# Values in tiles of 128 tokens, sent through DRAM, in the window attention of a four-layer image kernel

## The chip, the cores and the metric

The kernel runs on one core of one Trainium2 chip. The metric is the device time of one execution in microseconds (us), as a median over several runs. A core has several engines that run side by side and meet only at semaphores: TensorE (PE) for matmuls, VectorE (DVE), ScalarE (ACT), GpSimd (POOL), and SyncE (SP), whose queue here issues the transfers (DMA) between the memory of the chip (DRAM) and the core's own SBUF. Matmuls write to PSUM, which has eight banks. The profile shows PE's weight loads as a line of their own (PEld), and a float32 matmul as two records.

## The reference

Four images of 56 x 56 tokens with 256 channels go through four layers. Each adds to its input an attention-like function of the group-normalised input. Only layer 3 is touched by this change. It is an attention in windows of 7 x 7 tokens, on an image shifted by 3:

```python
xs = jnp.roll(x, (-3, -3), axis=(1, 2))
xw = (windows of 7 x 7).reshape(B * nW, 49, C)
qkv = xw @ qkv_weight.T + qkv_bias            # q, k, v: 8 heads of 32
attn = softmax(q * 32**-0.5 @ k.T + bias + mask)
out = (attn @ v) @ proj_weight.T + proj_bias
```

then windows and shift are undone and the result is added to `x`. Queries, keys and values of a token are a product of its 256 normalised channels with a 256 x 256 matrix each.

## The kernel before

The stream of activations lies in DRAM with channels first, and each layer reads it and writes the next. In layer 3 the unit of work is a row of eight windows: 8 x 49 = 392 tokens (`WC`), eight rows an image, 32 rows in all. All is float32, with the channels in two halves of 128 (`CC = 2`). What happens to a row `r`:

- `load` and `prepare(r)`: the row is loaded, and DVE normalises it (`normalise`, L940) into `xn`, permuted so that the tokens of a window are next to each other. Six small operations.
- `project_rows(r)`: keys and queries come from `project` (L946), with the weights held in PE and 392 tokens streamed past them; ACT empties their PSUM tiles (L1841, L1845). Values are made the other way round by `value_rows` (L963): 98 tokens, a pair of windows, are held as weights and the 256 columns of the value matrix are streamed, so that a pair's values have their tokens on partitions 0 to 97. Four such pieces a row, two to a PSUM tile; DVE adds the bias and writes them to `v` (L965).
- `quad(r, hq)`, two for a row, one for each four heads. In `attend_quads` a unit's `logits` (L998) go into PSUM; DVE adds the mask to one half of them (L1003), ACT takes exponentials (L1002, L1004), POOL multiplies the other half by its exponentiated mask (L1005). One unit later `products` (L1013) multiply by `v` and by ones. After that `done` divides: a reciprocal (L1864) and a scaling (L1866) on DVE.
- `project_out(r)`, two rows later: `project` with `w_p`, ACT adds the bias into `pr` (L1886), POOL adds it to the old `x` in `xr` (L1888), and the row is stored (`transfer`, L1801).

The order is written out by hand: layer 3 runs under a manual schedule in which PE, DVE, ACT and POOL take their instructions in the order of the program. Only SP's queue is ordered by the scheduler. The loop over units is

```python
for w in units:
    logits(w)
    done()
    w["fill"]()
    if held:
        products(held)
        done = held["done"]
    held = w
```

so that between the logits of a unit and the products of the one before, PE is given the filling work of `stream()`: for each half `hq` of row `r` one step of the output projection of row `r - 2`, then three of the six steps of `project_rows(r + 1)` (keys, queries, values, in this order), and in the second half `prepare(r + 2)`.

PSUM is full: logits take two tiles of two banks, products one of two banks, and all that goes through `ps_m` (projections, values, statistics) shares two tiles of one bank, which are given out in turn.

Of the kernel before, what the change touches and what calls it, by code (L numbers as in the profile page):

```python
# [24 lines left out]
FP = mybir.dt.float32  # L25
I32 = mybir.dt.int32
AF = mybir.ActivationFunctionType
ALU = mybir.AluOpType
# [3 lines left out]
NIMG = 4  # L32
S = 56
T = S * S
C = 256
P = 128
CC = C // P
HD = 32
# [10 lines left out]
WC = 8 * WN  # L49
# [782 lines left out]
def direct_blocks(ctx: ExitStack, tc: tile.TileContext, d: dict, watch):  # L832
# [3 lines left out]
    nc = tc.nc  # L836
    const = ctx.enter_context(tc.tile_pool(name="dconst", bufs=1))
    dram = ctx.enter_context(tc.tile_pool(name="ddram", bufs=1, space=bass.MemoryType.DRAM))
# [8 lines left out]
    def tokens_of(l, b, t0, n):  # L847
        return stream_of[l][b].rearrange("(h p) t -> p h t", p=P)[:, :, t0:t0 + n]
# [7 lines left out]
    bv0, bv2, bv3, baff, gamma, beta = (bc[:, i, :] for i in range(6))  # L856
# [14 lines left out]
    def psum_tile(tag, bufs, banks=1):  # L871
        shape = [P, 512] if banks == 1 else [P, banks, 512]
        return ps.tile(shape, FP, tag=tag, name="ps_" + tag, bufs=bufs)
# [3 lines left out]
    def ps_m():  # L877
        return psum_tile("m", m_bufs)
# [55 lines left out]
    def known(l, b):  # L934
        while (l, b) not in stats:
            pending.pop(0)()
        return stats[l, b]

    def normalise(dst, src, gst, h):
        nc.vector.tensor_scalar(dst, src, gst[:, h, 0:1], gst[:, h, 1:2], ALU.subtract, ALU.mult)  # L940
# [16 lines left out]
    def value_rows(v, a, n, xn, w, bias):  # L957

        pm = ps_m()
        for j in range(2):  # L960
            k = 2 * a + j
            for h in range(CC):
                nc.tensor.matmul(pm[:n, j * C:(j + 1) * C], lhsT=xn[:, h, k * n:(k + 1) * n],  # L963
                                 rhs=w[:, h, :], start=(h == 0), stop=(h == CC - 1))
        nc.vector.tensor_tensor(v[:, 2 * a:2 * a + 2, :], pm[:n, :].rearrange("p (j c) -> p j c", c=C),  # L965
                                bias[:n].rearrange("p (o c) -> p o c", o=1).to_broadcast([n, 2, C]), ALU.add)

    def seen(rs):

        w = watch[0][:, :rs.shape[1]]  # L970
        nc.gpsimd.tensor_tensor(w, w, rs, ALU.add)
# [129 lines left out]
    def lazily(make, i, n):  # L1101

        made = []
        return [lambda k=k: (made or made.extend(make(i)), made[k]()) for k in range(n)]
# [687 lines left out]
    def layer3(early, big, pool, brief):  # L1792
        def image_rows(wr):

            return [(0, 7, 7 * wr + 3)] if wr < 7 else [(0, 4, S - 4), (4, 3, 0)]

        def transfer(l, r, x, out):
            b, wr = divmod(r, 8)
            for i0, n, r0 in image_rows(wr):
                ends = x[:, :, i0 * S:(i0 + n) * S], tokens_of(l, b, r0 * S, n * S)  # L1800
                nc.sync.dma_start(out=ends[out], in_=ends[1 - out])  # L1801

        xs, xns, qkv, attns = {}, {}, {}, {}

        def load(r):
            xs[r] = early.tile([P, CC, WC], FP, tag="x", name="x3")
            transfer(3, r, xs[r], 0)

        load(0)
        w_qkv = weight(early, "wqkv3", 3 * C)  # L1810
        m3 = big.tile([98, 2, NH, 4 * 98], FP, name="m3l")
        nc.sync.dma_start(out=m3, in_=m3d.rearrange("p a h w k -> p a h (w k)"))
        w_p = weight(pool, "wp3", C)

        def parts(win, x):

            win = win.rearrange("p (w i j) -> p w i j", i=7, j=7)
            img = x.rearrange("p (r c) -> p r c", c=S)
            yield (win[:, 0:7].rearrange("p w i j -> p i w j"), img[:, :, 3:52].rearrange("p r (w j) -> p r w j", j=7))
            yield win[:, 7, :, 0:4], img[:, :, 52:56]  # L1820
            yield win[:, 7, :, 4:7], img[:, :, 0:3]

        def prepare(r):
            x = xs.pop(r)
            if r + 1 < NIMG * 8:
                load(r + 1)
            xn = xns[r] = early.tile([P, CC, WC], FP, tag="xn", name="xn3")
            for h in range(CC):
                for w, xv in parts(xn[:, h, :], x[:, h, :]):
                    normalise(w, xv, known(3, r // 8), h)  # L1830

        def project_rows(r):
            xn = xns.pop(r)
            qT = pool.tile([P, CC, WC], FP, tag="q", name="q3")
            kT = pool.tile([P, CC, WC], FP, tag="k", name="k3")
            v = pool.tile([98, 4, C], FP, tag="v", name="v3")
            qkv[r] = qT, kT, v

            def keys(m):
                pm = project(w_qkv, C + m * P, lambda h: xn[:, h, :], WC)  # L1840
                nc.scalar.activation(kT[:, m, :], pm, AF.Identity, bias=bk3[:, m:m + 1])  # L1841

            def queries(m):
                pm = project(w_qkv, m * P, lambda h: xn[:, h, :], WC)
                nc.scalar.activation(qT[:, m, :], pm, AF.Identity, bias=qbias[:, 2, m:m + 1], scale=SCALE)  # L1845

            def values(a):
                value_rows(v, a, 98, xn, w_qkv[:, :, 2 * C:], bv3)

            return [lambda f=f, m=m: f(m) for m in range(2) for f in (keys, queries, values)]  # L1850

        def quad(r, hq):
            b, wr = divmod(r, 8)
            qT, kT, v = qkv[r]
            box = {}

            def output(k, u):
                if k + u == 0:
                    box["o"] = psum_tile("o", 1, 2)
                return box["o"][:, k, u * 98:(u + 1) * 98]  # L1860

            def finish():
                rs = pool.tile([P, WC], FP, tag="rs", name="rs3")
                nc.vector.reciprocal(rs, box["o"][:, 1, :WC])  # L1864
                seen(rs)
                nc.vector.scalar_tensor_tensor(attns[r][:, hq, :], box["o"][:, 0, :WC], 1.0, rs, ALU.mult, ALU.mult,  # L1866
                                               accum_out=watch[2][:, 2 * r + hq:2 * r + hq + 1])

            def piece(u):
                sl = slice(u * 98, (u + 1) * 98)  # L1870
                return (lambda j: kT[hr(j), hq, sl], lambda j: qT[hr(j), hq, sl],
                        lambda j: v[:, u, (4 * hq + j) * HD:(4 * hq + j + 1) * HD], True, True)

            mk = m3[:, wr // 7, 4 * hq:4 * hq + 4, :]
            i = 2 * (NIMG * 8 + r) + hq
            return dict(pieces=[piece(u) for u in range(4)], nk=98, nq=98, width=WC, mask=mk[:, 0:2, :],
                        emask=mk[:, 2:4, :], sum=watch[2][:98, i:i + 1], o=output, first=no_step, done=finish)

        def project_out(r):
            x = pool.tile([P, CC, WC], FP, tag="xr", name="xr3")  # L1880
            transfer(3, r, x, 0)

            def step(m):
                pm = project(w_p, m * P, lambda h: attns[r][:, h, :], WC)
                pr = pool.tile([P, WC], FP, tag="pr", name="pr3")
                nc.scalar.activation(pr, pm, AF.Identity, bias=bp3[:, m:m + 1])  # L1886
                for w, xv in parts(pr, x[:, m, :]):
                    nc.gpsimd.tensor_tensor(xv, xv, w, ALU.add)  # L1888
                if m:
                    transfer(4, r, x, 1)  # L1890
            return [lambda m=m: step(m) for m in range(CC)]

        def stream():
            n = NIMG * 8
            for r in range(n):
                attns[r] = pool.tile([P, CC, WC], FP, tag="attn", name="attn3", bufs=3)
                rows = lazily(project_rows, r + 1, 6) if r + 1 < n else []
                out = project_out(r - 2) if r > 1 else []
                for hq in range(CC):
                    steps = out[hq:hq + 1] + rows[3 * hq:3 * hq + 3]  # L1900
                    if hq and r + 2 < n:
                        steps.append(lambda r=r: prepare(r + 2))
                    steps.append(step_stats)
                    w = quad(r, hq)
                    w["fill"] = lambda steps=steps: [f() for f in steps]
                    yield w

        prepare(0)
        prepare(1)
        for step in project_rows(0):  # L1910
            step()
        attend_quads(pool, stream())
        for r in range(NIMG * 8 - 2, NIMG * 8):
            for step in project_out(r):
                step()
# [114 lines left out]
```

## Time and profile before

| | |
|---|---|
| time, median of 3 runs | 4114.57 us (4113.07 to 4121.27) |
| span of the profiled execution | 4109.9 us |
| PE, DVE, ACT, POOL busy | 95%, 58%, 33%, 42% of the span |
| first logits of layer 3 | at 3567.07 us |
| one half of a row in layer 3's steady part | 8.25 us |
| value matmuls (L963), layers 2 and 3 | 1024 records, 250.0 us busy |

Layer 3 takes about the last 540 us. A line of a group or of the timeline names the line in the kernel, the engine, the operation, what is written and read with shapes, and then how long and how often. In square brackets, or after a second bar, stands how long the engine stood idle just before and whose end released it. The time on PE of a group in the timeline includes the tail of its last matmul, so distances between starts say more than the lengths.

### The profile page before, as it was taken

The numbers are of one execution on the slowest core, as the hardware profiler recorded it, in microseconds if no ns is written. First come the engines' busy times: TensorE is split into PE (matmuls) and PEld (weight loads), VectorE is DVE, ScalarE is ACT, GpSimd is POOL, SyncE is SP. The second block draws the span as 40 slices with busy tenths as digits, with TensorE's granted clock in tenths as the row PEclk, the third lists the DMA queues.
The fourth block names the chain that finished last, engine by engine and source line by source line (L and its number), as shares of the span: only waits on it lengthen the run. The fifth ranks groups of instructions, "written<-read, shape, count | busy, mean of one in ns | idle before, by whom it ended". The sixth has DMA issues, their size and how long they took to land. (4 is left out here: it accounts for less than half of the span.)

```text
span 4109.9 us, 92570 instructions
## 1 busy us (share of the span) xinstructions
PE 3910.4 (95%) x39191; PEld 2788.9 (68%) x39191; DVE 2381.8 (58%) x4437; ACT 1373.1 (33%) x2850; POOL 1741.2 (42%) x1883
## 2 busy tenths in 40 slices
PE   6899999899999999999999999997999999899998
PEld 4566666577777677776777677775666666666665
DVE  6777777734345434454344533444688887666665
ACT  2444545422222122221222212222554555444443
POOL 2566667621123211242112411123676777554544
PEclk9999999999999999999999999998999999999999
DMA  7344333210000100000000000003344443322221
GB/s 261 101 133 122 113 112 101 89 41 10 15 15 24 34 9 15 15 29 29 10 15 15 28 17 10 10 19 117 109 127 121 123 122 112 104 76 73 72 76 61
DMA packets 239794, 275.89 MB, mean 67 GB/s; under 512 B 22150, under 2 KB 231720, under 8 KB 238888
## 3 DMA queue, kind: packets, MB, share of 16 engines
q1 hardware_dynamic: 239082, 269.80, 21.1%
q8 instruction: 310, 5.08, 0.5%
q14 instruction: 114, 0.93, 0.1%
q10 hardware_dynamic: 288, 0.08, 0.0%
HBM read 190.29 MB, written 79.53 MB: 66 GB/s over the span
## 5 line engine op out<-in xcount | busy, mean ns | idle before, releaser
L1414 DVE TENSOR_TENSOR acc<-acc,ps_v 128x257 f32<-128x257 f32 x1104 | 457.2, 421 | 679.5 <-PE ps_v L1410 676.6
L1410 PE MATMUL ps_v<-xw,e 128*128 128x257 f32 x2400 | 666.4, 382 | 27.4 <-DVE acc L1414 17.2
L1405 PE MATMUL ps_o<-xw,at 128*128 128x257 f32 x2400 | 662.5, 380 | 0.0
L1377 PE MATMUL ps_s<-xnT,xd 128*128 128x512 f32 (+3 forms) x1456 | 622.0, 550 | 5.1 <-DVE xnT L1359 5.1
L1410 PEld LDWEIGHTS ps_v<-xw,e 128*128 128x128 f32 x2400 | 445.1, 189 | 193.2 <-issue 91.8
L1394 ACT COPY at<-ps_t 128x512 f32<-128x512 f32 (+3 forms) x360 | 184.8, 513 | 1054.4 <-PE ps_t L1391 1054.4
L1064 POOL TENSOR_TENSOR b<-e 126x336 f32<-126x336 f32 (+5 forms) x512 | 499.7, 997 | 12.1 <-ACT e L1052 4.1
L1405 PEld LDWEIGHTS ps_o<-xw,at 128*128 128x128 f32 x2400 | 455.5, 190 | 65.3
L1370 POOL TENSOR_SCALAR xd<-xnT,vec 128x128 f32<-128x128 f32 x200 | 122.2, 622 | 707.4 <-PE ps_s L1377 705.6
L946 PE MATMUL ps_m<-xn,w_wqkv 128*128 128x392 f32 x1024 | 375.5, 500 | 3.3 <-DVE xr L1693 2.5
L1055 POOL TENSOR_TENSOR e<-e,m0t 126x672 f32<-126x672 f32 (+3 forms) x128 | 238.7, 1865 | 280.7 <-ACT e L1054 267.9
L1377 PEld LDWEIGHTS ps_s<-xnT,xd 128*128 128x128 f32 x1456 | 245.1, 191 | 155.6 <-issue 138.8
L1055 POOL TENSOR_TENSOR e<-e,bias 119x784 f32<-119x784 f32 (+5 forms) x128 | 244.5, 1911 | 215.7 <-ACT e L1054 214.8
L1380 ACT ACTIVATE e<-ps_s 128x512 f32<-128x512 f32 (+3 forms) x364 | 200.8, 552 | 375.2 <-PE ps_s L1377 373.3
L976 ACT ACTIVATE no<-rs 128x168 f32<-128x168 f32 (+2 forms) x256 | 93.8, 367 | 624.7 <-DVE rs L1658 283.1
L1073 PEld LDWEIGHTS ps_o<-e,vp 124*32 124x32 f32 (+3 forms) x8192 | 177.1, 111 | 142.9 <-issue 93.5
L946 PEld LDWEIGHTS ps_m<-xn,w_wqkv 128*128 128x128 f32 x1024 | 188.2, 190 | 124.8 <-ACT pr L1886 17.3
L963 PE MATMUL ps_m<-w_wqkv,xn 128*98 128x256 f32 x1024 | 250.0, 388 | 8.2 <-DMA w_wqkv<-in_wqkv 7.0
L1073 PE MATMUL ps_o<-e,vp 124*32 124x112 f32 (+3 forms) x8192 | 240.2, 254 | 6.2 <-POOL e L1055 4.7
L940 DVE TENSOR_SCALAR xn<-x,gst 128x28 f32<-128x28 f32 (+5 forms) x368 | 204.8, 611 | 50.7 <-PE ps_m L946 26.9
L1052 ACT ACTIVATE e<-e 126x672 f32<-126x672 f32 (+5 forms) x256 | 219.4, 857 | 24.0 <-DVE e L1051 10.7
L965 DVE TENSOR_TENSOR v<-ps_m,bc 98x512 f32<-98x512 f32 (+1 forms) x184 | 126.2, 686 | 174.3 <-PE ps_m L963 98.3
(164 smaller groups left out, 6136.4 us busy)
## 6 DMA issues: line engine op xcount, KB each, us to landing
x<-xr SPq DMA_DIRECT2D x64, 392.0 KB
x<-in_x SPq DMA_DIRECT2D x53, 448.0 KB
xr<-x SPq DMA_DIRECT2D x60, 392.0 KB
x<-x SPq DMA_DIRECT2D x60, 392.0 KB
vd<-v SPq DMA_DIRECT2D x28, 448.0 KB
xr<-in_x SPq DMA_DIRECT2D x32, 392.0 KB
xr<-x SPq DMA_DIRECT2D x28, 448.0 KB
x<-xr SPq DMA_DIRECT2D x28, 448.0 KB
```

The source lines that it names most:

```text
L940: nc.vector.tensor_scalar(dst, src, gst[:, h, 0:1], gst[:, h, 1:2], ALU.subtract, ALU.mult)
L946: nc.tensor.matmul(pm[:, :n], lhsT=w[:, h, col:col + P], rhs=rhs(h), start=(h == 0), stop=(h == CC - 1))
L963: nc.tensor.matmul(pm[:n, j * C:(j + 1) * C], lhsT=xn[:, h, k * n:(k + 1) * n], rhs=w[:, h, :], start=(h == 0), stop=(h == CC - 1))
L1052: nc.scalar.activation(ev, ev, AF.Exp)
L1055: nc.gpsimd.tensor_tensor(parts(ev), parts(ev), w["emask"], ALU.mult)
L1064: nc.gpsimd.tensor_tensor(w["b"][a][:nk, :, :2 * nq].rearrange("p h (i c) -> p h i c", i=2), ev[:, :, :, 0, :], ev[:, :, :, 1, :], ALU.add)
L1073: nc.tensor.matmul(w["o"](k, i)[j * HD:(j + 1) * HD], lhsT=ones[:nk, :HD] if k else v(j, u), rhs=w["b"][j // 2][:nk, j % 2, i * nq:(i + 1) ...
L1377: nc.tensor.matmul(s[:, :n], lhsT=xd[j][:, h, :], rhs=xnT[:, h, first * P:last * P], start=(h == 0), stop=(h == CC - 1))
L1380: nc.scalar.activation(e[:, :n], s[:, :n], AF.Exp, scale=5.0)
L1405: nc.tensor.matmul(out[j][:, :C + 1], lhsT=e[:, col(i)] if i == j else at[:, col(i)], rhs=xw[:, i, :], start=(i == j), stop=(i == NB - 1))
L1410: nc.tensor.matmul(pv[:, :C + 1], lhsT=e[:, col(i)], rhs=xw[:, j, :], start=True, stop=True)
L1414: nc.vector.tensor_tensor(acc[:, i, :], acc[:, i, :], pv[:, :C + 1], ALU.add)
```

## The change

Values are no longer made for each pair of windows but for tiles of 128 tokens, which fill the 128 columns of PE's weights. Since a row has 392 tokens, which isn't a multiple of 128, the tiles run on over the rows of an image: 25 for 3136 tokens, the last of 64. What a row leaves over (`left`: up to 120 tokens) is copied by ACT to the front of the next row's `xn`, which grows to 448 tokens and to three buffers. A tile of values has other tokens on its partitions than a pair of windows needs, so it is stored to a DRAM buffer `vd3` by token, and `gather` loads a row back as four pairs of 98 tokens into `v`. To leave time for this, values are made two rows ahead in place of one, and rows are prepared three ahead.

The filling work of a half changes in order as well: one step of the output projection, then one step of values (for row `r + 2`), then keys and queries (for row `r + 1`). The tile of values, `vt`, has one buffer. The core of the diff:

```diff
+    def value_tiles(v, a, c, n, xn, w, bias, dst):
+        t0, t1 = c * n // P, (c + 1) * n // P if (c + 1) * n < T else -(-T // P)
+        pm = ps_m()
+        sizes = [min(P, T - t * P) for t in range(t0, t1)]
+        mine = sizes[2 * a:2 * a + 2]
+        for j, k in enumerate(mine):
+            first = (2 * a + j) * P
+            for h in range(CC):
+                nc.tensor.matmul(pm[:k, j * C:(j + 1) * C], lhsT=xn[:, h, first:first + k], rhs=w[:, h, :],
+                                 start=(h == 0), stop=(h == CC - 1))
+        for k in sorted(set(mine)):
...
+            nc.vector.tensor_tensor(
...
+            nc.sync.dma_start(out=dst[t * P:min((t + len(js)) * P, T), :].rearrange("(k p) c -> p k c", p=k),
...
-            xn = xns[r] = early.tile([P, CC, WC], FP, tag="xn", name="xn3")
+            xn = xns[r] = early.tile([P, CC, 448], FP, tag="xn", name="xn3", bufs=3)
...
+            if at:
+                end = left(c - 1, WC) + WC
+                nc.scalar.copy(xn[:, :, :at], ahead[0][:, :, end - at:end])
...
-            return [lambda f=f, m=m: f(m) for m in range(2) for f in (keys, queries, values)]
+            return [lambda f=f, m=m: f(m) for m in range(2) for f in (keys, queries)]
+
+        def gather(r):
+            b, c = divmod(r, 8)
+            vs[r] = pool.tile([98, 4, C], FP, tag="v", name="v3")
+            nc.sync.dma_start(out=vs[r], in_=vd[b][c * WC:(c + 1) * WC, :].rearrange("(k p) c -> p k c", p=98))
+
+        def values(r):
...
+            v = pool.tile([P, 4, C], FP, tag="vt", name="vt3", bufs=1)
+            def step(a):
+                value_tiles(v, a, c, WC, xn, w_qkv[:, :, 2 * C:], bv3, vd[b])
+                if a == 0 and r:
+                    gather(r - 1)
...
-                    steps = out[hq:hq + 1] + rows[3 * hq:3 * hq + 3]
-                    if hq and r + 2 < n:
-                        steps.append(lambda r=r: prepare(r + 2))
+                    steps = out[hq:hq + 1] + ahead_values[hq:hq + 1] + rows[2 * hq:2 * hq + 2]
+                    if hq and r + 3 < n:
+                        steps.append(lambda r=r: prepare(r + 3))
...
         prepare(0)
         prepare(1)
+        for r in range(2):
+            for step in values(r):
+                step()
         for step in project_rows(0):
             step()
+        prepare(2)
         attend_quads(pool, stream())
```

More of the change, by code (lines that the diff above doesn't have):

```diff
@@ L966, in value_rows, with left @@
                                 bias[:n].rearrange("p (o c) -> p o c", o=1).to_broadcast([n, 2, C]), ALU.add)
+    def left(c, n):
+        return c * n % P
+    def value_tiles(v, a, c, n, xn, w, bias, dst):
[9 more added lines that the diff above has]
+        for k in sorted(set(mine)):
+            js = [j for j, kj in enumerate(mine) if kj == k]
+            nc.vector.tensor_tensor(
+                v[:k, 2 * a + js[0]:2 * a + js[-1] + 1, :], pm[:k, js[0] * C:(js[-1] + 1) * C].rearrange("p (j c) -> p j c", c=C),
+                bias[:k].rearrange("p (o c) -> p o c", o=1).to_broadcast([k, len(js), C]), ALU.add)
+            t = t0 + 2 * a + js[0]
+            nc.sync.dma_start(out=dst[t * P:min((t + len(js)) * P, T), :].rearrange("(k p) c -> p k c", p=k),
+                              in_=v[:k, 2 * a + js[0]:2 * a + js[-1] + 1, :])
     def seen(rs):
@@ L1801, in transfer @@
                 nc.sync.dma_start(out=ends[out], in_=ends[1 - out])
-        xs, xns, qkv, attns = {}, {}, {}, {}
+        xs, xns, vs, qk, attns, ahead = {}, {}, {}, {}, {}, []
+        vd = [dram.tile([T, C], FP, name=f"vd3_{b}") for b in range(NIMG)]
         def load(r):
@@ L1826, in prepare @@
                 load(r + 1)
-            xn = xns[r] = early.tile([P, CC, WC], FP, tag="xn", name="xn3")
+            c = r % 8
+            xn = xns[r] = early.tile([P, CC, 448], FP, tag="xn", name="xn3", bufs=3)
+            at = left(c, WC)
             for h in range(CC):
-                for w, xv in parts(xn[:, h, :], x[:, h, :]):
+                for w, xv in parts(xn[:, h, at:at + WC], x[:, h, :]):
                     normalise(w, xv, known(3, r // 8), h)
+            if at:
+                end = left(c - 1, WC) + WC
+                nc.scalar.copy(xn[:, :, :at], ahead[0][:, :, end - at:end])
+            ahead[:] = [xn]
         def project_rows(r):
-            xn = xns.pop(r)
+            at = left(r % 8, WC)
+            xn = xns.pop(r)[:, :, at:at + WC]
             qT = pool.tile([P, CC, WC], FP, tag="q", name="q3")
             kT = pool.tile([P, CC, WC], FP, tag="k", name="k3")
-            v = pool.tile([98, 4, C], FP, tag="v", name="v3")
-            qkv[r] = qT, kT, v
+            qk[r] = qT, kT
             def keys(m):
@@ L1845, in queries @@
                 nc.scalar.activation(qT[:, m, :], pm, AF.Identity, bias=qbias[:, 2, m:m + 1], scale=SCALE)
-            def values(a):
-                value_rows(v, a, 98, xn, w_qkv[:, :, 2 * C:], bv3)
-            return [lambda f=f, m=m: f(m) for m in range(2) for f in (keys, queries, values)]
+            return [lambda f=f, m=m: f(m) for m in range(2) for f in (keys, queries)]
[4 more added lines that the diff above has]
+        def values(r):
+            b, c = divmod(r, 8)
+            xn = xns[r]
+            v = pool.tile([P, 4, C], FP, tag="vt", name="vt3", bufs=1)
[3 more added lines that the diff above has]
+                    gather(r - 1)
+                if a and r == NIMG * 8 - 1:
+                    gather(r)
+            return [lambda a=a: step(a) for a in range(2)]
         def quad(r, hq):
             b, wr = divmod(r, 8)
-            qT, kT, v = qkv[r]
+            qT, kT = qk[r]
             box = {}
@@ L1871, in piece @@
                 return (lambda j: kT[hr(j), hq, sl], lambda j: qT[hr(j), hq, sl],
-                        lambda j: v[:, u, (4 * hq + j) * HD:(4 * hq + j + 1) * HD], True, True)
+                        lambda j: vs[r][:, u, (4 * hq + j) * HD:(4 * hq + j + 1) * HD], True, True)
             mk = m3[:, wr // 7, 4 * hq:4 * hq + 4, :]
@@ L1896, in stream @@
                 attns[r] = pool.tile([P, CC, WC], FP, tag="attn", name="attn3", bufs=3)
-                rows = lazily(project_rows, r + 1, 6) if r + 1 < n else []
+                rows = lazily(project_rows, r + 1, 4) if r + 1 < n else []
+                ahead_values = lazily(values, r + 2, 2) if r + 2 < n else []
                 out = project_out(r - 2) if r > 1 else []
                 for hq in range(CC):
-                    steps = out[hq:hq + 1] + rows[3 * hq:3 * hq + 3]
-                    if hq and r + 2 < n:
-                        steps.append(lambda r=r: prepare(r + 2))
+                    steps = out[hq:hq + 1] + ahead_values[hq:hq + 1] + rows[2 * hq:2 * hq + 2]
+                    if hq and r + 3 < n:
+                        steps.append(lambda r=r: prepare(r + 3))
                     steps.append(step_stats)
```

## The prediction

> **What bounds the kernel now.** I went from the whole to the one stage that the change touches. The page says that TensorE (PE) is busy 95% of the span. Busy time alone says little for a pipelined engine, so I cut out layer 3, which begins at about 3567 us, with the view by windows, once in its steady part and once at its end.
>
> ```profile
> PE 3910.4 (95%) x39191; PEld 2788.9 (68%) x39191; DVE 2381.8 (58%) x4437; ACT 1373.1 (33%) x2850; POOL 1741.2 (42%) x1883
> ```
> ```profile
> 3603.11:4072.00 468.89, 468.89 (x6576) 319.71 (x6576) 315.15 (x453) 195.20 (x342) 233.72 (x285) 1.00 0.22 72
> 4072.00:4110.00 38.00, 17.39 (x302) 11.73 (x290) 15.96 (x20) 6.84 (x12) 15.18 (x24) 0.83 0.21 66
> ```
>
> For 469 us PE has no idle time at all, at full clock (1.00), while VectorE (DVE) has 315 us of work and the DMA engines are 22% busy. So layer 3 is bound by the number and length of its matmuls. One half of a row (one step of the stream, one `hq`) in the timeline of PE, then the same stretch on DVE; columns are start, length, engine, line, operation, count, and the idle time before with what ended it:
>
> ```profile
> 3602.24 0.95 PE L998 MATMUL ps_s<-q,k 32*98 32x98 f32 x32
> 3603.11 1.58 PE L946 MATMUL ps_m<-attn,w_wp 128*128 128x392 f32 x4
> 3604.53 2.80 PE L946 MATMUL ps_m<-xn,w_wqkv 128*128 128x392 f32 x8
> 3607.17 1.89 PE L963 MATMUL ps_m<-w_wqkv,xn 128*98 128x256 f32 x8
> 3608.99 0.89 PE L1013 MATMUL ps_o<-e,v 98*32 98x98 f32 x32
> ```
> ```profile
> 3603.29 0.97 DVE L1003 TENSOR_TENSOR e<-ps_s,m3l 98x784 f32<-98x784 f32 x1 [0.90 <-PE ps_s L998]
> 3604.18 2.60 DVE L1864 RECIPROCAL rs<-ps_o 128x392 f32<-128x392 f32 x1
> 3606.81 0.56 DVE L1866 SCALAR_TENSOR_TENSOR attn<-ps_o,rs 128x392 f32<-128x392 f32 x1
> 3607.30 0.08 DVE L1866 DVE_READ_ACCUMULATOR attn<-ps_o,rs 128x1 f32 x1
> 3609.09 0.69 DVE L965 TENSOR_TENSOR v<-ps_m,bc 98x512 f32<-98x512 f32 x1 [1.71 <-PE ps_m L963]
> ```
>
> Call L the moment when the filling work begins on PE (3603.11 here). PE does output projection (L to L+1.42), keys and queries (to L+4.06), values (to L+5.88); then products and the next logits take 2.37, and the half is 8.25 us long. DVE, in the order written, does the mask, the reciprocal, the scaling of the previous unit (through at L+4.27), and only then the bias-add that empties the values' PSUM tile. Today the values come last on PE, at L+5.88, so DVE is long free: it waits 1.71 us for PE, not PE for it.
>
> Two more views. The waits, in the same stretch:
>
> ```profile
> PEld ps_m L946 <- ACT pr L1886: 17.0, 57, 0.3
> ```
>
> That is the queries' first weight load waiting until the output projection's tile, two back in `ps_m`, is emptied: the two buffers go round in turn, and the third project of a half waits for the first. And the last row, which has no filling work but the output projection:
>
> ```profile
> 4073.17 1.58 PE L946 MATMUL ps_m<-attn,w_wp 128*128 128x392 f32 x4
> 4077.59 0.89 PE L1013 MATMUL ps_o<-e,v 98*32 98x98 f32 x32 [2.83 <-DVE attn L1866]
> ```
>
> There L is 4073.17, and PE stands still until L+4.42 for the very DVE chain above. So this chain is only some 1.5 us away from being the bound.
>
> **What the Trainium skill says.** "Perfetto Trace Analysis", Sequencer Loop: an instruction of an engine goes into that engine's queue and there waits for its semaphore. In this trace what stands behind it in program order waits too (the 2.83 us above). The same page, Identifying Performance Opportunities, says that a gap repeating on the engine that should be saturated can mean that SBUF or PSUM had no room for the next tile. The trace of before shows the seed of it, the 0.3 us on `ps_m`. "TensorE: Matmul & The Clock Gate", LDWEIGHTS: a weight load's time goes with its columns. The trace agrees: 165 ns for 98 columns, 190 for 128. Both are below the 216 ns of a 256-wide matmul record with 128-column weights (L1349 in layer 1: 8 in 1.73 us), so wider tiles cost PE nothing each.
>
> **The change, part by part.**
>
> 1. Fewer value matmuls. An image has 32 pieces of 98 tokens now and 25 tiles of 128 afterwards, with two matmuls (two records each) per piece. That removes 14 matmuls an image, 56 in all. One is 2 x 213 ns (8 records in 1.71 us), so PE has 56 x 0.427 = 24 us less to do. By row: 3 tiles in place of 4, two in the first half and one in the second; each eighth row keeps 4.
>
> 2. The order in the filling. Values now stand second, right behind the output projection, and keys and queries follow. With two `ps_m` buffers, keys take over the output's tile and queries that of the values. So queries wait for DVE's bias-add, which DVE, in order, can't start before L+4.27. Behind that wait on PE stand queries, then products, then the next logits, hence the next mask and reciprocal: the loop closes, and the wait comes in every half.
>  - First half: values matmuls end at about L+3.1, keys at L+4.45. Bias-add L+4.26 to L+4.95 (98x512 took 0.69). A released weight load starts 0.06 later (layer 2's releases by DVE show that). Queries after a stop take 1.42, as the output projection does after logits, to L+6.43; with the 0.11 that PE now loses going into the products, the filling ends at L+6.54 instead of L+5.88: +0.66 us.
>  - Second half: one tile of 256, whose add I take from layer 1's 128x257 at 421 ns. 4.26 + 0.42 + 0.06 + 1.42 + 0.11 = L+6.27: +0.39 us.
>  - A row: +1.05 us, with the saved matmuls already inside, since the wait swallows them. Rows 2 to 29 do this: 28 x 1.05 = 29.4. In four rows the second half makes two tiles, of 128 and 64 tokens, with two adds of about 0.4: 4 x 0.34 = 1.4.
>
> 3. The ends. Row 0 has no previous unit in its halves at first, so no reciprocal ahead of the add, and gains its second half's tile: -0.9. Row 1 has no output projection yet, so its filling is 4.86 us now (half 7.23) and 6.54 and 6.27 afterwards: +3.1. Row 30 makes no values any more and becomes like the last row, L+4.42 instead of 5.88, twice: -2.9. Before the stream, two rows of values are made instead of one. The second row's tile has one buffer (`bufs=1`), so its first add waits until the first row's store has landed; I take 3.7 us for that, as an `xr` load of layer 2 near its end does. The first logits then start at about 3571.3 instead of 3567.07: +4.2.
>
> 4. DMA. Each row stores up to 512 KB and loads 392 KB back. Stores in layer 3 take 2.6 to 4.2 us to land (the queue's waits for `out_x`). A store goes out at L+5, the next row's add into the same buffer is due one half (9 us) later or more. The load is issued more than a half before its first use. Traffic doubles from 22% busy. So I cost it at nothing: attention's matmuls of the next halves hide it. The queue itself waits in order, and a store may stand behind the output's, which waits for GpSimd; that goes into the range.
>
> 5. The copy of left-over tokens: 28 copies on ScalarE of at most 128x240; a 128x512 copy there took 513 ns (L1394), so under 0.5 us each. ScalarE is busy 195 of 469 us and does it after the queries' eviction: nothing. The third `xn` buffer and normalising one row earlier move work without adding any. DVE's old wait for products before it may overwrite `v` (2.56 us in every other half) goes, but it held up no one on PE.
>
> Sum: 29.4 + 1.4 - 0.9 + 3.1 - 2.9 + 4.2 = +34 us. 4114.6 + 34 = 4149 us.
>
> **The rivals.**
>
> A. PE's count alone decides (the order does no harm, the DMA is hidden). That needs queries free by L+4.45. For it: 469 us without idle. Against it: the DVE chain shown by the last row, and only two `ps_m` buffers. Time: 4114.6 - 24 + 4 (start) = 4095. Chance 0.09.
>
> B. As forecast, and the one-buffer value tile bites as well: the store is stuck behind the output's store in the DMA queue, and each row's first add waits about 1 us more. For it: the queue waits 345 us for GpSimd's `xr` in layer 3. Against it: a full half of slack. 30 rows x 1 us more: 4179. Chance 0.12.
>
> C. The stall is smaller than worked out, with PE making up part of it, and the two cancel: within 8 us of before, at 4115. It would need the add to start 0.7 us sooner in both halves. Chance 0.05.
>
> **How the numbers follow.** My forecast has 0.74. Its own spread is that of the half (0.2 us each way, 60 halves: 12 us) and of the start (2 us less if the store lands at once). The range 4118 to 4172 takes that and the near side of B, and leaves out A, C and the far side of B. Faster 0.09, same 0.05, slower the rest, 0.86.
>
> **What would show it.** Right: in the steady part of layer 3 a half is 8.9 and 8.7 us by turns, PE idles 0.4 to 0.9 us in each, ended mostly by the values' bias-add on DVE ahead of an L946 matmul; value records in layer 3 fall from 512 to 400. Step 4 right: no DVE wait on a DMA of `vd`. Wrong: halves of 8.25 and 7.4 us (A), DVE's bias-add waiting for the store (B), or a long wait ahead of the first products for `v3`.

## The result: slower by 0.75%

| | before | after |
|---|---|---|
| median of 6 runs | 4113.82 us (4104.31 to 4121.27) | 4144.27 us (4137.72 to 4150.95) |
| ratio, 95% interval | | 1.0075 (1.0059 to 1.009) |
| first logits of layer 3, in the profile | 3567.07 | 3573.68 |
| from these to the last logits | 512.0 | 538.8 |
| from the last logits to the end | 30.8 | 29.3 |

The profile after, in the same two views as before. First a window of the steady part of layer 3, in the kernel before and then after (stretch, its length, then busy time and count for PE, PEld, DVE, ACT and POOL, then granted clock, DMA share and GB/s):

```profile
3620.00:4050.00 430.00, 430.00 (x6037) 293.20 (x6036) 289.40 (x418) 179.22 (x315) 213.57 (x261) 1.00 0.23 74
```
```profile
3620.00:4050.00 430.00, 405.28 (x5600) 263.38 (x5600) 274.65 (x392) 170.15 (x314) 202.62 (x245) 1.00 0.38 116
```

PE now idles for 24.7 of 430 us at full clock, in a stretch in which it never stood still before. In this window it had 6037 matmul records done before and has 5600 now; the value records that are saved explain only a part of that. Second, a row on PE. The first six lines are a second half (L is 3697.94), the next five the first half of the row after it (L is 3706.66); L983 is the line of the value matmuls now:

```profile
3697.94 1.58 PE L946 MATMUL ps_m<-attn,w_wp 128*128 128x392 f32 x4
3699.36 1.03 PE L983 MATMUL ps_m<-w_wqkv,xn 128*128 128x256 f32 x4
3700.51 1.58 PE L946 MATMUL ps_m<-xn,w_wqkv 128*128 128x392 f32 x4
3702.77 1.58 PE L946 MATMUL ps_m<-xn,w_wqkv 128*128 128x392 f32 x4 [0.68 <-ACT k L1874]
3704.29 0.89 PE L1039 MATMUL ps_o<-e,v 98*32 98x98 f32 x32
...
3705.78 0.95 PE L1024 MATMUL ps_s<-q,k 32*98 32x98 f32 x32
3706.66 1.58 PE L946 MATMUL ps_m<-attn,w_wp 128*128 128x392 f32 x4
3708.08 1.89 PE L983 MATMUL ps_m<-w_wqkv,xn 128*128 128x256 f32 x8
3709.81 1.48 PE L946 MATMUL ps_m<-xn,w_wqkv 128*128 128x392 f32 x4
3711.59 1.58 PE L946 MATMUL ps_m<-xn,w_wqkv 128*128 128x392 f32 x4 [0.30 <-DVE vt L987]
3713.10 0.89 PE L1039 MATMUL ps_o<-e,v 98*32 98x98 f32 x32
```

Queries, the fourth group of each half, wait. In the first half DVE's bias-add releases them at L+4.93, in the second ACT's eviction of the keys, at L+4.83. The DVE queue in the first half shows why the add comes so late:

```profile
3706.83 0.97 DVE L1029 TENSOR_TENSOR e<-ps_s,m3l 98x784 f32<-98x784 f32 x1 [2.13 <-PE ps_s L1024]
3707.72 2.60 DVE L1914 RECIPROCAL rs<-ps_o 128x392 f32<-128x392 f32 x1
3710.36 0.57 DVE L1916 SCALAR_TENSOR_TENSOR attn<-ps_o,rs 128x392 f32<-128x392 f32 x1
3710.85 0.08 DVE L1916 DVE_READ_ACCUMULATOR attn<-ps_o,rs 128x1 f32 x1
3710.85 0.69 DVE L987 TENSOR_TENSOR vt<-ps_m,bc 128x512 f32<-128x512 f32 x1
```

The values' matmuls are through at L+3.2, but the add stands fifth in its queue, behind a reciprocal of 2.60 us, without a gap between them. The halves are 8.82 and 8.72 us by turns, 17.54 us for a row that took 16.49. In every eighth row the second half makes two tiles and takes 8.94. What PE's weight loads (PEld) and its matmuls (PE) waited for in the window, in total, times and the longest:

```profile
PEld ps_m L946 <- ACT k L1874: 27.4, 21, 1.3
PEld ps_o L1039 <- issue: 27.4, 49, 0.6
PEld ps_m L946 <- DVE vt L987: 23.3, 25, 1.0
PE ps_m L946 <- ACT k L1874: 14.2, 21, 0.7
PEld ps_m L946 <- ACT pr L1936: 11.0, 21, 0.5
PE ps_m L946 <- DVE vt L987: 7.6, 25, 0.3
```

So of PE's own standing still ahead of queries, 14.2 us are ended by ACT and only 7.6 us by DVE.

Of the waits of PE and DVE in the same window none names a transfer. (The 0.56 us on average that weight loads stand ahead of `ps_o` are there in the third experiment too, 27.4 us in 49 times, where values don't go through DRAM.) Only the DMA queue itself waits, 44.1 us in 22 times, for stores to `vd` to land before it loads from it. So the way through DRAM holds up no engine here, though DMA is 38% busy in place of 23% in the same window before, and the page counts 12.84 MB more read and as much more written.

### The profile page after: what moved, and what is told of

Same layout as the page of the kernel before. It is cut to its first block, busy times and chain, and to the rows that moved or that the text cites. A ratio compares the mean times of both kernels' runs of the same rounds, so it can differ in the third digit from the quotient of the medians.

```text
span 4141.8 us, 92542 instructions
## 1 busy us (share of the span) xinstructions
PE 3915.4 (95%) x39079; PEld 2776.8 (67%) x39079; DVE 2387.8 (58%) x4441; ACT 1377.4 (33%) x2878; POOL 1743.1 (42%) x1883
## 5 line engine op out<-in xcount | busy, mean ns | idle before, releaser
L946 PE MATMUL ps_m<-xn,w_wqkv 128*128 128x392 f32 x1024 | 391.8, 507 | 32.1 <-ACT k L1874 17.6
L940 DVE TENSOR_SCALAR xn<-x,gst 128x28 f32<-128x28 f32 (+4 forms) x368 | 221.0, 653 | 47.6 <-PE ps_m L946 26.9
L1031 POOL TENSOR_TENSOR e<-e,m3l 98x784 f32<-98x784 f32 x64 | 118.2, 1847 | 269.0 <-ACT e L1028 269.0
L1684 DVE RECIPROCAL rs<-ps_o 128x196 f32<-128x196 f32 (+2 forms) x128 | 176.0, 1375 | 86.6 <-PE ps_o L1099 86.1
```

The source lines that it names most:

```text
L946: nc.tensor.matmul(pm[:, :n], lhsT=w[:, h, col:col + P], rhs=rhs(h), start=(h == 0), stop=(h == CC - 1))
L1684: nc.vector.reciprocal(rs.rearrange("p (t c) -> p t c", t=2), pv[:, :, 1, :])
```

## The experiments

The theory: it is the place of the values in the filling that costs the time. The rival: the way through DRAM does, with its stores, loads, copies and the one buffer that a store must leave.

**Values last.** The changed kernel with one line different:

```diff
-steps = out[hq:hq + 1] + ahead_values[hq:hq + 1] + rows[2 * hq:2 * hq + 2]
+steps = out[hq:hq + 1] + rows[2 * hq:2 * hq + 2] + ahead_values[hq:hq + 1]
```

> The changed kernel with one edit: the values' step stands last in the filling again (output projection, keys, queries, values). Theory (the order makes queries wait for a tile of PSUM that DVE empties late): no wait before queries; halves of 8.25 and about 7.4 us by turns, 24 us of matmuls saved less about 4 to 7 us at the start of layer 3, so 4090 to 4097 us, faster than before. Rival (the way through DRAM, its copies and its transfers cost the time): stays at about 4144 us, halves of 8.8 and 8.7 us.

Measured: 4087.98 us, ratio to the kernel before 0.994 (0.992 to 0.9961). This is 2 us below the range that was expected. A second half on PE, the start of the half after it, and the window of the steady part:

```profile
3706.06 1.58 PE L946 MATMUL ps_m<-attn,w_wp 128*128 128x392 f32 x4
3707.48 2.80 PE L946 MATMUL ps_m<-xn,w_wqkv 128*128 128x392 f32 x8
3710.11 1.03 PE L983 MATMUL ps_m<-w_wqkv,xn 128*128 128x256 f32 x4
3711.07 0.89 PE L1039 MATMUL ps_o<-e,v 98*32 98x98 f32 x32
...
3713.45 1.58 PE L946 MATMUL ps_m<-attn,w_wp 128*128 128x392 f32 x4
```
```profile
3620.00:4050.00 430.00, 429.80 (x6222) 298.29 (x6224) 294.85 (x433) 190.35 (x351) 228.71 (x273) 1.00 0.42 127
```

The waits are gone, PE is idle for 0.2 of 430 us, and the half shown takes 7.39 us. With the same transfers, the same copies and the same one buffer, the kernel is 56 us faster than the changed one. The rival falls for the steady part.

**Values third.** The same kernel with the values between keys and queries:

```diff
+steps = out[hq:hq + 1] + rows[2 * hq:2 * hq + 1] + ahead_values[hq:hq + 1] + rows[2 * hq + 1:2 * hq + 2]
```

> The changed kernel with the values' step between keys and queries. Theory: queries now take the tile of the keys, which ACT empties 1.1 us before queries are due, and the tile of the values is asked for only in the next half; so no wait either, 4090 to 4097 us, as with values last. If it were simply bad to have values ahead of queries, it would be as slow as the changed kernel, about 4144 us.

Measured: 4097.98 us, 0.9963 (0.9951 to 0.9976), a us above what was expected and far from 4144. First halves are 8.25 us as with values last; second halves are 7.47 in place of 7.38, and there the queries' weight loads now wait up to 0.2 us for the keys' eviction. That makes 3.4 us from the first to the last logits (491.1 against 487.7); the spans of the two profiled executions differ by 3.1 us, while the 10 us between the medians rest on four and eight runs. So being ahead of queries does next to no harm if another project stands between the output projection and the values. What counts is whose tile the queries take over and when that is empty.

**The old kernel with values second.** This leaves out DRAM, wide tiles and copies, and keeps the order alone:

```diff
-v = pool.tile([98, 4, C], FP, tag="v", name="v3")
+v = pool.tile([98, 4, C], FP, tag="v", name="v3", bufs=3)
...
-return [lambda f=f, m=m: f(m) for m in range(2) for f in (keys, queries, values)]
+return [lambda f=f, m=m: f(m) for m in range(2) for f in (values, keys, queries)]
```

> The kernel before, with its pieces of 98 tokens and no DRAM, but values first among the row's steps (output projection, values, keys, queries), and a third buffer of v, without which the order couldn't run. Theory: both halves have a 98x512 add ahead of queries, filling 6.54 in place of 5.88 us, 29 rows x 2 x 0.66 + 3 for row 1 = +42 us, about 4156 us. Rival (DRAM route): as before, 4114 us.

Measured: 4145.79 us, 1.0082 (1.0058 to 1.0107). The same wait as in the changed kernel, in both halves:

```profile
3705.10 1.48 PE L946 MATMUL ps_m<-xn,w_wqkv 128*128 128x392 f32 x4
3706.89 1.58 PE L946 MATMUL ps_m<-xn,w_wqkv 128*128 128x392 f32 x4 [0.30 <-DVE v L965]
```

The order by itself makes the kernel slower, by 31 us in the medians and by 34.9 us in the profiles, from the first to the last logits. That is less than the 42 expected: a half is 8.82 us, +0.57 and not +0.66, and row 1 grew by 1.4 and not by 3.

**DVE's chain lengthened.** One more operation right ahead of the bias-add in the DVE queue, in the changed kernel and in the one before. Nothing reads its output:

```diff
 accum_out=watch[2][:, 2 * r + hq:2 * r + hq + 1])
+more = pool.tile([P, WC], FP, tag="more", name="more3", bufs=1)
+nc.vector.tensor_tensor(more, rs, rs, ALU.add)
```

In the changed kernel:

> The changed kernel with one addition more on DVE (128x392, about 0.5 us) after the scaling of a unit, so ahead of the values' bias-add in the DVE queue. Theory: in the first half, where the add ends the wait, the half grows by the whole 0.5 us; in the second half, where the trace names the keys' eviction by ACT as the release, two readings: if queries there need the values' tile too, the add passes ACT by about 0.35 us and the half grows by that; if they take the keys' tile, it doesn't grow. So +27 us or +16 us on 4144. Rival (DRAM route): no change, since nothing in it waits for that operation.

Measured: 4156.02 us, 1.0093 (1.0076 to 1.011) against the kernel before, so 12 us above the changed one by the medians; neither +27 nor +16 came out. The operation took 1.05 us, not 0.5, and still the first half grew only by 0.37 (8.82 to 9.19). The second stayed at 8.72. A first half (L is 3699.61), on DVE and on PE:

```profile
3703.79 1.05 DVE L1919 TENSOR_TENSOR more<-rs 128x392 f32<-128x392 f32 x1
3704.77 0.68 DVE L987 TENSOR_TENSOR vt<-ps_m,bc 128x512 f32<-128x512 f32 x1
```
```profile
3702.75 1.48 PE L946 MATMUL ps_m<-xn,w_wqkv 128*128 128x392 f32 x4
3704.91 1.58 PE L946 MATMUL ps_m<-xn,w_wqkv 128*128 128x392 f32 x4 [0.68 <-ACT k L1874]
```

The add ends at 3705.45, and queries started half a us earlier, so they can't be in the values' tile: they are in the keys'. That tells the two readings of the second half apart, and corrects one premise of the prediction. It also means that this run doesn't measure what a later add costs, since the longer chain moved the queries of the first half to another tile. The programs that the kernels are built into say the same. The bank of PSUM that each project of a half is given, in the order of PE:

```
                            output  values  keys  queries
changed, first half            0       1      0      1
changed, second half           0       1      0      0
changed, DVE longer, both      0       1      0      0
old, values second, both       0       1      0      1
```

(The numbers 0 and 1 are exchanged in every other row or so; which projects share one is what matters. The second line holds for 24 of the 28 second halves of rows 2 to 29; the four with two tiles of values are like the first line. In the kernel before, where keys and queries come ahead of the values, the four go strictly by turns.) So the two tiles are not always given out in turn. The table fits a planner that takes the one that it reckons will be free first; how it reckons was not looked into. In the changed kernel's first half queries get the values' tile, in most of the second halves, and in all halves after the lengthening, the keys'.

In the kernel before:

> The kernel before with the same addition. Theory: the DVE chain then ends at L+4.8, still 1 us before the products need it at L+5.88, and the values' add comes after its matmuls anyway: no change, 4114 us within 0.2%.

Measured: 4112.17 us, 0.9997 (0.9986 to 1.0008). The same microsecond of work on DVE costs nothing where the bias-add isn't waited for.

**Values last, and two buffers of `vt`.** On top of the first experiment:

```diff
-v = pool.tile([P, 4, C], FP, tag="vt", name="vt3", bufs=1)
+v = pool.tile([P, 4, C], FP, tag="vt", name="vt3", bufs=2)
```

> Values last and two buffers of vt. Theory: the second row's values at the start no longer wait for the first row's store (PE stood 2.6 us there in the changed kernel), and nothing else changes: 2 to 4 us less than with values last alone, about 4090 us. If the store held up something in the steady part as well, it would be more.

Measured: 4090.66 us, 0.9938 (0.9917 to 0.9958), the same as with one buffer within what these runs can tell; the 2 to 4 us that were expected don't show in the medians. The profile tells more. At the start of layer 3 the changed kernel has this on PE and DVE:

```profile
3557.41 8.25 PE L983 MATMUL ps_m<-w_wqkv,xn 128*128 128x256 f32 x24 [4.00 <-DVE xr L1719]
3568.22 5.54 PE L946 MATMUL ps_m<-xn,w_wqkv 128*128 128x392 f32 x16 [2.55 <-DVE vt L987]
```
```profile
3567.47 1.02 DVE L987 TENSOR_TENSOR vt<-ps_m,bc 128x512 f32<-128x512 f32 x2 [4.11 <-DMA vd<-vt]
```

and with two buffers PE goes through:

```profile
3555.21 7.69 PE L983 MATMUL ps_m<-w_wqkv,xn 128*128 128x256 f32 x24 [5.12 <-DVE xr L1719]
3562.82 5.53 PE L946 MATMUL ps_m<-xn,w_wqkv 128*128 128x392 f32 x16
```

From PE's first value matmul to the first logits it is 13.08 us in place of 16.27. (With values last and one buffer it was 17.99 us: a wait of 2.94 us for the same add, and keys and queries at a granted clock of 0.76.) The halves are 8.25 and 7.38 us as with one buffer, so in the steady part the second buffer is worth nothing.

## Why the prediction was right

The forecast was 4149 us in a range of 4118 to 4172; 4144 came out. The mechanism is the one that was forecast, queries that wait for a tile of PSUM behind a late eviction, but in most of the second halves the tile and the engine that empties it are others. That the number is so close is in part luck: there the keys' eviction happens to end within 0.2 us of the add that was reckoned with, and an error in the stream cancels one at the start. By its steps:

1. Fewer matmuls: right. Value records of layer 3 are 395 in the profile (400 were forecast), and eight of them take 1.89 us with 128 columns as they did with 98. The weight load rises from 165 to 190 ns, by less than the columns do. Once the order lets the saved matmuls count, they bring their 24 us: with values last the stretch from first to last logits is 487.7 us, against 512.0.

2. The order: right, and shown by four kernels. It costs 31 us in the old kernel alone and, undone, gives 56 us back in the new one. Rows 2 to 29 took 30.2 us more than before, 30.8 were forecast. Two terms were off in opposite ways. The first half grew by 0.57 and not 0.66: the add starts together with the reading of the accumulator (L+4.19) and not 0.07 after it, and queries and the step into the products take 1.51 us. The second half grew by 0.47 and not 0.39, because queries are in the keys' tile and wait for ACT. (In the four rows with two tiles it is DVE again, and +0.69 where 0.73 was forecast.) The keys begin only when the output projection's tile is empty (the 0.5 us of `pr` in the waits above), and their eviction ends at L+4.78, a little after the add.

 The premise that failed is therefore "the two buffers go round in turn". It held in every half of the trace it was read from. In the new order it fails in 24 of the 56 halves of rows 2 to 29. So the sign that was named, idle time of PE ended mostly by the bias-add, came out only by a little in the count (25 of 46 waits) and not in the time (7.6 of 21.8 us). The wait stayed, since with two buffers queries must follow either values or keys, and both are emptied late.

3. The ends: the stream, from first to last logits, was forecast 3.3 us too high (30.1 against 26.8), mostly by row 1, and the start 3.2 us too low. Row 0 gave -0.9 and row 30 gave -2.9, as forecast. Row 1 gave +0.6 in place of +3.1, by the same premise: without an output projection keys come early, and queries wait 0.7 us for ACT instead of for DVE. The start cost 7.35 us in place of 4.2 (16.27 against 8.92 from PE's first matmul to the first logits). The store that had to land is 2.55 of it, and eight more value records are 1.7. The rest is that the 24 value records took 8.25 us where 5.1 would be their share, with a granted clock of 0.65 over that stretch. Before it was 1.00 there. Not counted in this is that PE stood still for 4.00 us ahead of layer 3 where it had been 2.55, until DVE had added up the last rows of layer 2. In the three kernels without tiles of 128 it was 2.5 to 2.8 us, in the five with them 4.0 to 7.1. In the kernel before DVE waits there for a load of layer 2 (`xr<-x`, 3.22 us). In the changed kernel, where the trace names no releaser for the 4.35 us, the loads of two rows of layer 3 go out right behind that load; whether they slow it was not tried.

4. DMA: right for the steady part. Neither PE nor DVE waited for a transfer of `vd` there, and the second buffer of `vt` changed nothing. Its share didn't double but rose from 23% to 38%. Rival B falls. Whether the traffic cost something at the start is open (see 3).

5. The copies: right. They took 6.4 us of ACT (L1862, 27 in the profile), behind the queries' eviction.

Rival A, PE's count alone, forecast 4095 us. It is what the change is worth in another order: 4088 and 4098.

## What to carry to other kernels

When work on a saturated engine is reordered, write down for each PSUM tile who empties it, when that instruction's turn comes in its own queue, and which later matmul takes the tile over. A matmul group whose tile is emptied behind a long operation did best last in its batch here, where its wait falls into work that needs no tile from the same pool. And before a detour through DRAM is blamed or dropped, try it in an order that doesn't add a wait: here the same detour is 30 us slower or 26 us faster than the kernel before, by one line.

## What the runs showed of the hardware that was not expected

The added operation, a tile of 128x392 in SBUF added to itself, took 1.05 us on DVE, while the scaling of the same shape, with one operand in PSUM, took 0.57 and the bias-add of 128x512, with one operand in PSUM, 0.69. Two operands in SBUF are not enough to explain it: another such addition (L1773 in the kernel before, 98x392) took 0.55 us, the median of 8. What makes the added one slow was not tried.

PE's granted clock at the start of layer 3 went with how long PE had stood still ahead of it. After 2.5 to 2.8 us, in the three kernels without tiles of 128, it was 1.00 over the next 9 us. After 4.0 to 7.1 us, in the five with them, it was 0.64 to 0.70 over the 24 value records, which took 7.7 to 8.4 us. After the second stop, for the store, it was 1.00 where that took 2.4 to 2.8 us (three kernels) and 0.76 after 2.94 us (values last). What sets it was not tried.
